# Position terms of queries and keys as sums of a row part and a column part, made on GpSimd, in the head of an attention kernel

## The chip, the cores and the metric

The kernel runs on one core of one Trainium2 chip. The core has five engines that run side by side, each through its own list of instructions in order: TensorE (PE, matrix products into PSUM), VectorE (DVE), ScalarE (ACT), GpSimd (POOL) and SyncE (SP, which here only issues DMAs). The metric is device microseconds from start to end of one execution; the median of several executions is the time of a kernel.

## The reference, cut to what matters

The input x is 8 images of 128 channels by 48 × 48 pixels, N = 2304 positions. Layer 0 normalises each image by groups of channels, appends 32 position channels to the 128 channels, and makes queries, keys and values with one linear map each and a leaky rectifier. Causal attention over the 2304 positions follows, its result is added to x. Layer 1 is a second attention without a mask on normalised tokens, and then a recurrent feed-forward part.

```python
pe = _pos_embeddings(S)            # 32 x 48 x 48: px depends on the row alone, py on the column alone
x0 = concatenate([_gn(x), pe], axis=1).reshape(B, C + 32, N)
q = lrelu(einsum('kc,bcn->bkn', Wq, x0) + bq[None, :, None])
k = lrelu(einsum('kc,bcn->bkn', Wk, x0) + bk[None, :, None])
v = lrelu(einsum('vc,bcn->bvn', Wv, x0) + bv[None, :, None])
attn = einsum('bkn,bkm->bnm', q, k) / sqrt(128)
...
x = x + out1                       # then layer 1: full attention, feed-forward, recurrence
```

The linear map over 160 channels splits into one over the 128 image channels and one over the 32 position channels and the bias. The second is the same for all 8 images. It is called the position term here. In a position channel the value depends either on the row of the pixel or on its column, so the position term at pixel (r, w) is

term(r, w) = term(r, 0) + term(0, w) − term(0, 0).

## The kernel before

**Tiling.** An image is held as a tile of 128 channels × 2304 positions. It is worked through in NQ = 6 chunks of QC = 384 positions (8 rows of 48 pixels). All numbers are fp32. One matrix product in the program appears in the profile as two MATMUL records, each with its own weight load (LDWEIGHTS, engine PEld), so that a count of x2 there is one product.

**The head.** Before the first image's attention can start, the program loads x (L716, three pieces of two chunks each through `load_x`), the position channels `pe` with a row of ones (33 rows, in two halves `pe_sb[0]` and `pe_sb[1]`) and the weights. PE starts with 12 products of the identity matrix with itself (`idle`, L1505), whose result nobody reads. They keep PE busy until the first data is there. `group_norm` computes the mean and variance of the image in three parts: BATCH_NORM_STATS2 of each chunk as x arrives (L805), then a product that averages over the channels of a group (L813), then a second such product for the variance (L824) and the reciprocal root on POOL (`rsqrt`, L669). Only then can DVE normalise the first chunk (xn, L892), and PE can multiply it by the weights (pj, L899 and L902).

**Position terms.** `positions(n, j)` makes the position term of chunk n for queries (j = 0), keys (j = 1) or values (j = 2). For j < 2 it is one product of 33 rows with 384 columns (L847). For j = 2, where the layout is turned, it is three products of 128 columns (L850). ACT copies the result from PSUM to an SBUF tile `pb` (L851). After j = 2 the whole tile is also stored to DRAM as `posb_d` (L853), from where images 1 to 7 load it. So these 18 steps are done once, in the head. Chunk 0 comes before the statistics of x, the terms of chunk 1 for q and k come behind the variance product, and chunks 2 to 5 are the steps of a chain called `making`.

**Projection.** `project(b, n)` is a chain of steps: normalise a chunk (L892), then for q, k and v a product into PSUM (L899, L902), an addition of the position term on DVE (L906), and the leaky rectifier on DVE (L907). A last step measures the largest q and k (L921).

**Attention.** For each chunk of queries and each block of 128 keys there is a product s (L1038), the exponential on ACT (L1040), for blocks on the diagonal a multiplication by the triangle mask on POOL (`triu`, L1043), and a product o with the values (L1049), which is issued LAG = 3 blocks later. DVE sums the exponentials (L1060, L1064).

**What sets the order.** The program is written under a manual schedule: the instructions of each engine run in the order of the Python calls. A planner (`Stream`) decides that order. It holds chains of steps, each with a cost on PE and a list of costs on other engines, and keeps a clock `st.now` that every product moves forward. After each attention block `st.tick()` runs up to two steps whose planned time has come. `st.advance` and `st.finish` run a chain's steps at once. An engine waits at each instruction for its inputs and for a free buffer, and everything behind it on that engine waits too. PSUM tiles called `s` have four buffers, and tiles called `t` two.

Of the kernel before, what the change touches and what calls it, by code (L numbers as in the profile page):

```python
# [14 lines left out]
F32 = mybir.dt.float32  # L15
AF = mybir.ActivationFunctionType
# [6 lines left out]
NPE = 2 * EMB  # L23
# [581 lines left out]
def fast_path(ctx: ExitStack, tc: tile.TileContext, x, pe, w_ffn, out, x_tok, w_qkv, w_pos, v_t, gamma_beta, flag):  # L605
    nc = tc.nc
    B, C, H, W = x.shape
    N = H * W
    P = 128
# [3 lines left out]
    QC = 384  # L613
    NQ = N // QC
    QB = QC // P
    SCALE = 1.0 / math.sqrt(P)
    US = 4 / 2400.0
# [10 lines left out]
    wx = cpool.tile([P, LS, B, SEGS], F32, tag="wx", name="wx")  # L628
# [42 lines left out]
    with ExitStack() as actx:  # L671
# [16 lines left out]
        def psum_s(name):  # L688
            return ps_s.tile([P, CH], F32, tag="s", name=name)

        def psum_t(name):
            return ps_t.tile([P, CH], F32, tag="t", name=name)
# [19 lines left out]
        def load_x(b, pieces=(3, 3)):  # L712
            xbuf[b] = big.tile([P, N], F32, tag="x", name=f"x_{b}")
            at = 0
            for n in pieces:
                nc.sync.dma_start(xbuf[b][:, ds(at, n * QC)], x_v[b, :, ds(at, n * QC)])  # L716
                at += n * QC

        load_x(0, (2, 2, 2))


        cg = C // GROUPS
# [67 lines left out]
        st = Stream()  # L790
# [7 lines left out]
        def group_norm(b):  # L798
            xt = xbuf[b]
            c = {}  # L800

            def part1():
                gs = small2.tile([P, NQ, 6], F32, tag="gn_st", name=f"gn_st_{b}")
                for j in range(NQ):
                    nc.vector.bn_stats(gs[:, j, :], xt[:, ts(j, QC)])  # L805
                mv = small2.tile([P, 2], F32, tag="gn_mv", name=f"gn_mv_{b}")
                nc.vector.bn_aggr(mv, gs)
                c["mv"] = mv

            def part2():  # L810
                mv = c["mv"]
                tp = psum_t(f"gn_m_{b}")
                nc.tensor.matmul(tp[:, 0:1], grp, mv[:, 0:1], start=True, stop=True)  # L813
                mg = small2.tile([P, 1], F32, tag="gn_mg", name=f"gn_mg_{b}")
                nc.vector.tensor_copy(mg, tp[:, 0:1])
                d = small.tile([P, 1], F32, tag="gn_d", name=f"gn_d_{b}")
                nc.vector.tensor_sub(d, mv[:, 0:1], mg)
                e = small2.tile([P, 1], F32, tag="gn_e", name=f"gn_e_{b}")
                nc.vector.scalar_tensor_tensor(e, d, d, mv[:, 1:2], ALU.mult, ALU.add)
                c["mg"], c["e"] = mg, e  # L820

            def part3():
                tp = psum_t(f"gn_v_{b}")
                nc.tensor.matmul(tp[:, 0:1], grp, c["e"], start=True, stop=True)  # L824
                rs = small2.tile([P, 1], F32, tag="gn_rs", name=f"gn_rs_{b}")
                rsqrt(small2, rs, tp[:, 0:1], 1e-5, "gn")
                norm_of[b] = c["mg"], rs

            return [(part1, 0.0, [("DVE", 3.6), ("", 5.0 if b else 0.0)]), (part2, 0.15, [("DVE", 0.6), ("", 2.0 if b else 0.0)]), (part3, 0.15, [("DVE", 0.15), ("POOL", 0.9)])]
# [6 lines left out]
        def positions(n, j):  # L836

            if j == 0:
                if n > 3:
                    st.advance(projected[0, n - 4], 4)  # L840
                pool, tag = ((pbp, "pb"), (pbp, "pb"), (tpool, "t"), (gpool, "g"))[n % 4]
                tile_n = pool.tile([P, 3 * QC], F32, tag=tag, name=f"pb_0_{n}")
                pos[0, n] = made[n] = tile_n.rearrange("p (j c) -> p j c", j=3)
            pe_c = pe_sb[n // (NQ // 2)][: NPE + 1, ts(n % (NQ // 2), QC)]
            ps = psum_s(f"pb_{n}_{j}")
            if j < 2:
                nc.tensor.matmul(ps[:, :QC], wpT[: NPE + 1, j, :], pe_c, start=True, stop=True)  # L847
            else:
                for m in range(0, QC, P):
                    nc.tensor.matmul(ps[:, ds(m, P)], pe_c[:, ds(m, P)], wpT[: NPE + 1, j, :], start=True, stop=True)  # L850
            nc.scalar.copy(made[n][:, j, :], ps[:, :QC])  # L851
            if j == 2:
                nc.sync.dma_start(posb_d[:, n], made[n])  # L853

        def load_positions(b, n):
            def f():
# [645 lines left out]
        def idle(tp, n):  # L1502

            for _ in range(n):
                nc.tensor.matmul(tp[:, :P], ident, ident, start=True, stop=True)  # L1505

        idle(psum_s("idle"), 12)
        for j in range(3):
            positions(0, j)
        gn = st.add(group_norm(0))  # L1510
        idle(psum_s("idle_m"), 2)
        st.advance(gn, 2)
        idle(psum_s("idle_e"), 4)
        st.finish(gn)
        for j in range(2):
            positions(1, j)
        project(0, 0)
        st.advance(projected[0, 0], 4)
        st.advance(projected[0, 1], 1)
        positions(1, 2)  # L1520
        making = st.add([(partial(positions, n, j), QC * US, [("ACT", 0.5)]) for n in range(2, NQ) for j in range(3)], 6.0)


        LAG = 3
# [38 lines left out]
    with ExitStack() as rctx:  # L1563
# [91 lines left out]
        for t in range(-WARM, LS):  # L1655
            s = t % TZ
# [98 lines left out]
```

## Time and profile before

| what | value |
|---|---|
| median of 3 executions | 1719.08 us (1713.53, 1719.08, 1719.97) |
| profiled execution | 1715.02 us |
| its span in the profile | 1713.3 us |
| PE busy, share of span | 99% |
| DVE, ACT, POOL busy | 71%, 40%, 26% |
| granted PE clock | 0.995 of full speed |
| PE products L847 in the trace | 12 (24 records) |
| ACT copies L851 | 18, mean 478 ns |

How to read it: the span is the time from the first to the last instruction that the profile shows. The execution's time lies 1.7 us above it. A busy share of 99% on PE means that almost any work taken off PE in a stage where PE is busy shortens that stage, as long as nothing else is late. The table has no time by stage, so the head must be read from the timeline and from windows of the trace.

### The profile page before, as it was taken

The numbers are of one execution on the slowest core, as the hardware profiler recorded it, in microseconds if no ns is written. First come the engines' busy times: TensorE is split into PE (matmuls) and PEld (weight loads), VectorE is DVE, ScalarE is ACT, GpSimd is POOL, SyncE is SP. The second block draws the span as 40 slices with busy tenths as digits, with TensorE's granted clock in tenths as the row PEclk, the third lists the DMA queues.
The fourth block names the chain that finished last, engine by engine and source line by source line (L and its number), as shares of the span: only waits on it lengthen the run. The fifth ranks groups of instructions, "written<-read, shape, count | busy, mean of one in ns | idle before, by whom it ended". The sixth has DMA issues, their size and how long they took to land.

```text
span 1713.3 us, 22451 instructions
## 1 busy us (share of the span) xinstructions
PE 1687.8 (99%) x6259; PEld 1085.4 (63%) x6259; DVE 1209.1 (71%) x3297; ACT 684.8 (40%) x1300; POOL 449.9 (26%) x637
## 2 busy tenths in 40 slices
PE   9999999999999999999999999999999999999986
PEld 5666666666666666666666666666666666666665
DVE  5875578666886578865787568865798657974467
ACT  3344334433344324443244333443244442443355
POOL 1233122312133122322124112331213221341205
PEclk9999999999999999999999999999999999999998
DMA  3337763568445774368735684448743686347857
GB/s 122 101 89 210 225 200 109 131 193 251 129 129 145 238 230 128 79 189 244 205 101 130 199 252 139 125 130 244 227 146 71 176 244 207 81 96 211 237 221 223
DMA packets 316731, 291.67 MB, mean 170 GB/s; under 512 B 195793, under 2 KB 280690, under 8 KB 315956
## 3 DMA queue, kind: packets, MB, share of 16 engines
q1 hardware_dynamic: 306572, 268.76, 54.7%
q0 software_dynamic: 9792, 20.99, 4.5%
q8 instruction: 52, 0.85, 0.2%
q14 instruction: 83, 0.68, 0.1%
q10 hardware_dynamic: 232, 0.40, 0.1%
HBM read 164.13 MB, written 125.90 MB: 169 GB/s over the span
## 4 chain that ended last, share of the span: by engine, by line
PE 96%; DMA 2%; DVE 1%; SPq 0%; issue 0%; ACT 0%; DVEq 0%; ACTq 0%
PE s L1038 17%; PE s L1316 17%; PE o L1049 17%; PE o L1341 17%; PE o L1329 13%; PE pj L899 3%; PE pj L902 2%; PE o L1337 2%; PE z L1666 2%; PE wx L1424 2%; DMA g<-e 1%; PE of_t L957 1%; PE pb L847 0%; PE idle_last L1505 0%; DMA x<-in_x_dram 0%; DMA e<-t 0%
## 5 line engine op out<-in xcount | busy, mean ns | idle before, releaser
L1318 ACT ACTIVATE p<-s,shift 128x384 f32<-128x384 f32 (+2 forms) x504 | 274.2, 550 | 535.9 <-PE s L1316 436.8
L1040 ACT ACTIVATE p<-s 128x384 f32<-128x384 f32 (+2 forms) x504 | 229.4, 460 | 400.1 <-PE s L1038 323.6
L1038 PE MATMUL s<-q,k 128*128 128x384 f32 (+2 forms) x1008 | 380.6, 459 | 0.1
L1316 PE MATMUL s<-xh 128*128 128x384 f32 (+2 forms) x1008 | 379.2, 458 | 0.0
L1049 PE MATMUL o<-p,vT 128*128 128x384 f32 (+2 forms) x1008 | 377.5, 456 | 0.0
L1341 PE MATMUL o<-p,xhT 128*128 128x384 f32 (+2 forms) x1008 | 369.1, 456 | 0.0
L1281 DVE STREAM_TRANSPOSE t<-p 128x384 f32<-128x384 f32 x360 | 186.0, 553 | 170.8 <-DMA e<-t 106.3
L1329 PE MATMUL o<-g,xhT 128*128 128x384 f32 x720 | 282.2, 489 | 0.7 <-DMA g<-e 0.7
L1341 PEld LDWEIGHTS o<-p,xhT 128*128 128x128 f32 x1008 | 189.7, 190 | 120.3
L1049 PEld LDWEIGHTS o<-p,vT 128*128 128x128 f32 x1008 | 186.9, 190 | 109.9 <-POOL p L1043 2.0
L1316 PEld LDWEIGHTS s<-xh 128*128 128x128 f32 x1008 | 183.2, 191 | 99.6 <-issue 0.2
L1038 PEld LDWEIGHTS s<-q,k 128*128 128x128 f32 x1008 | 183.4, 190 | 99.0 <-issue 2.2
L1064 DVE TENSOR_TENSOR acc<-acc,p 128x384 f32<-128x384 f32 (+2 forms) x408 | 212.5, 521 | 23.1 <-DVE acc L1064 1.0
L1329 PEld LDWEIGHTS o<-g,xhT 128*128 128x128 f32 x720 | 132.6, 191 | 80.2 <-DMA g<-e 2.2
L1043 POOL TENSOR_TENSOR p<-p,triu 128x128 f32<-128x128 f32 x144 | 71.3, 497 | 356.1 <-ACT p L1040 355.8
L1266 POOL DMA_DIRECT2D gm<-m x192 | 105.3, 555 | 179.1 <-PE s L1316 63.2
L1262 POOL DMA_DIRECT2D m<-tm x48 | 29.9, 623 | 374.5 <-DVE tm L1249 374.5
L1138 POOL TENSOR_SCALAR xhT<-xhT 128x384 f32<-128x384 f32 x48 | 60.5, 1260 | 150.5 <-DVE yt L1150 121.2
L1249 DVE STREAM_TRANSPOSE tm<-p 128x256 f32<-128x256 f32 x96 | 33.9, 366 | 73.1 <-ACT p L1318 72.3
L899 PE MATMUL pj<-xn,wT 128*128 128x384 f32 x192 | 77.9, 488 | 1.5 <-DVE xn L892 1.5
L947 POOL TENSOR_TENSOR rs_c<-ve_c,mhalf 128x3 f32<-128x3 f32 x48 | 48.2, 1004 | 96.1 <-DVE ve_c L941 86.8
L906 DVE TENSOR_TENSOR q<-pj,pb 128x384 f32<-128x384 f32 x48 | 26.6, 554 | 50.1 <-PE pj L899 50.1
(256 smaller groups left out, 1681.1 us busy)
## 6 DMA issues: line engine op xcount, KB each, us to landing
e<-t SPq DMA_DIRECT2D x480, 144.0 KB
g<-e SPq DMA_DIRECT2D x120, 576.0 KB
pb<-posb_d SPq DMA_DIRECT2D x42, 576.0 KB
t1t<-in_x_tok_dram SPq DMA_DIRECT2D x48, 192.0 KB
m<-tm POOLq DMA_DIRECT2D x48, 192.0 KB, 4.3
gm<-m POOLq DMA_DIRECT2D x192, 48.0 KB, 3.8
t_d<-tt SPq DMA_DIRECT2D x184, 48.0 KB
t2x<-t_d SPq DMA_DIRECT2D x46, 192.0 KB
```

Source lines behind the costliest of these rows:

```text
L899: nc.tensor.matmul(ps[:, :QC], wT[:, j, :], xn, start=True, stop=True)
L1038: nc.tensor.matmul(s[:, off:QC], keys[b][:, ts(m, P)], queries[b, j][:, off:], start=True, stop=True)
L1040: nc.scalar.activation(p[:, off:], s[:, off:QC], AF.Exp, scale=SCALE)
L1043: nc.gpsimd.tensor_mul(p[:, off : off + P], p[:, off : off + P], triu)
L1049: nc.tensor.matmul(o[:, off:QC], vals[b][:, ts(m, P)], p[:, off:], start=first, stop=last)
L1064: nc.vector.tensor_add(a[:, off:], a[:, off:], p[:, off:])
L1266: nc.gpsimd.dma_start(gm[ts(r, SQ)].rearrange("c a q r -> c a (q r)"), d.rearrange("(a c) b f -> b c a f", a=R)[r])
L1281: nc.vector.transpose(t[:, :, :, g, :].rearrange("p b j r -> p j b r"), p.rearrange("p (j b r) -> p j b r", j=QB, b=R))
L1316: nc.tensor.matmul(s[:, off:QC], xh[:, ts(m, P)], xh[:, j * QC + off : (j + 1) * QC], start=True, stop=True)
L1318: nc.scalar.activation(p[:, off:], s[:, off:QC], AF.Exp, bias=shift)
L1329: nc.tensor.matmul(out_ap, xhT[:, QB * i + g, :], p, start=first, stop=last)
L1341: nc.tensor.matmul(o[:, off:QC], xhT[:, what[1], :], p[:, off:], start=first, stop=last)
```

## The change

`load_x` of the first image uses pieces of two, two, one and one chunks. A new function `separate` makes the parts of the sum, with PE products of 24 and 48 columns. Its results are kept in the beginning of the tile `wx`, which is otherwise first written by the feed-forward part of image 0. For chunks 1 to 5 and j < 2, `positions` no longer issues a product and a copy. It issues one addition on GpSimd, in which the row part is repeated along each row and the column part is repeated for each of the 8 rows. Chunk 0, and j = 2 of all chunks, stay as they were. The two idle products between the third `positions(0, j)` and the mean product (`idle_m`) go. Six idle products (`idle_r`) come behind the variance product. The calls of `positions` for q and k of chunks 1, 2 and 3 are moved ahead: chunk 1 ahead of the group norm, chunk 2 behind the variance, chunk 3 behind the first two projections. In `making`, the steps of chunks 4 and 5 with j < 2 cost nothing on PE and 1.0 us on POOL in the planner's account, and those of chunks 2 and 3 are empty.

```diff
-        load_x(0, (2, 2, 2))
+        load_x(0, (2, 2, 1, 1))
...
+            if j < 2 and n:
+                rows = by_row[:, j, ds((n - 1) * RC, RC)].unsqueeze(2).to_broadcast([P, RC, W])
+                columns = by_column[:, j, :].unsqueeze(1).to_broadcast([P, RC, W])
+                nc.gpsimd.tensor_add(made[n][:, j, :].rearrange("p (r w) -> p r w", w=W), rows, columns)
+                return
             pe_c = pe_sb[n // (NQ // 2)][: NPE + 1, ts(n % (NQ // 2), QC)]
...
+        RC = QC // W
+        flat = wx.rearrange("p l b s -> p (l b s)")
+        n = (NQ - 1) * RC
+        by_row = flat[:, : 2 * n].rearrange("p (j r) -> p j r", j=2)
+        by_column = flat[:, ds(2 * n, 2 * W)].rearrange("p (j w) -> p j w", j=2)
+
+        def separate(h):
+
+            ps = psum_t(f"pos_parts_{h}")
+            n = H // 2
+            parts = ps[:, : 2 * (n + W)].rearrange("p (j k) -> p j k", j=2)
+            for j in range(2):
+                first = pe_sb[h][: NPE + 1].rearrange("e (r w) -> e r w", w=W)[:, :, 0]
+                nc.tensor.matmul(parts[:, j, :n], wpT[: NPE + 1, j, :], first, start=True, stop=True)
+                if h == 0:
+                    nc.tensor.matmul(parts[:, j, n:], wpT[: NPE + 1, j, :], pe_sb[0][: NPE + 1, :W], start=True, stop=True)
+            if h:
+                nc.scalar.copy(by_row[:, :, n - RC :], parts[:, :, :n])
+                return
+            corner = small2.tile([P, 2], F32, tag="qk", name="pos_corner")
+            nc.scalar.activation(corner, parts[:, :, n], AF.Copy, scale=-1.0)
+            for j in range(2):
+                nc.scalar.activation(by_column[:, j, :], parts[:, j, n:], AF.Identity, bias=corner[:, j : j + 1])
+            nc.scalar.copy(by_row[:, :, : n - RC], parts[:, :, RC : n])
...
         idle(psum_s("idle"), 12)
+        separate(0)
         for j in range(3):
             positions(0, j)
+        for j in range(2):
+            positions(1, j)
         gn = st.add(group_norm(0))
-        idle(psum_s("idle_m"), 2)
         st.advance(gn, 2)
         idle(psum_s("idle_e"), 4)
         st.finish(gn)
+        idle(psum_s("idle_r"), 6)
         for j in range(2):
-            positions(1, j)
+            positions(2, j)
         project(0, 0)
         st.advance(projected[0, 0], 4)
+        separate(1)
         st.advance(projected[0, 1], 1)
         positions(1, 2)
-        making = st.add([(partial(positions, n, j), QC * US, [("ACT", 0.5)]) for n in range(2, NQ) for j in range(3)], 6.0)
+        for j in range(2):
+            positions(3, j)
+        def making_of(n, j):
+            if j == 2:
+                return partial(positions, n, j), QC * US, [("ACT", 0.5)]
+            return (partial(positions, n, j), 0.0, [("POOL", 1.0)]) if n > 3 else (lambda: None, 0.0, [])
+
+        making = st.add([making_of(n, j) for n in range(2, NQ) for j in range(3)], 6.0)
```

## The prediction

> **What bounds the kernel now.** I read the page first, then busy time by windows, then the chain of waits and the timeline of the first 60 us. The order of instructions in the changed kernel differs from the old one only in about the first 100 us; from there on it is the same on every engine. So the head alone decides. PE's line of the page (busy tenths in 40 slices of the span) and the windows (length; then PE, PE weight loads, DVE, ACT, POOL busy; granted clock; DMA share; GB/s):
>
> ```profile
> PE   9999999999999999999999999999999999999986
> ...
> 17.10:47.00 29.90, 29.85 (x114) 17.02 (x115) 16.92 (x38) 11.28 (x26) 3.87 (x8) 1.00 0.31 115
> 47.00:56.00 9.00, 8.30 (x35) 5.25 (x33) 8.54 (x26) 2.73 (x6) 1.32 (x2) 1.00 0.34 92
> 56.00:90.00 34.00, 33.78 (x123) 21.60 (x124) 32.17 (x86) 11.20 (x25) 10.32 (x12) 1.00 0.47 122
> ```
>
> From 17 to 47 us PE is never idle, while DVE is busy 57%, ACT 38%, POOL 13%. So PE bounds the stage that holds the products of chunks 2 to 5. From 47 us on DVE is busy 95% (8.54 of 9, 32.17 of 34), so little can go wrong there. The chain in that stage (start, length, what):
>
> ```profile
> 22.11 0.86 PE pb L850 x6
> 22.97 0.65 PE pb L847 x2
> 23.61 0.84 PE s L1038 x2
> 24.46 0.65 PE o L1049 x2
> 25.10 0.84 PE pb L847 x2
> 25.94 0.84 PE pj L899 x2
> 26.79 0.65 PE s L1038 x2
> ```
>
> A product of 384 columns takes 0.65. It takes 0.84 where it follows a product with another number of rows (33 after 128, or 128 after 33): 0.19 for the switch. The timeline's PE and POOL rows in the head (in brackets the idle time before a row and what ended it):
>
> ```profile
> 9.57 0.35 PE L813 MATMUL gn_m<-gn_mv,grp 128*128 128x1 f32 x2 [0.54 <-DVE gn_mv L807]
> 11.32 0.58 POOL L669 TENSOR_TENSOR gn_rs<-ve_gn,mhalf 128x1 f32<-128x1 f32 x1 [5.33 <-DVE ve_gn L668]
> 17.15 0.91 PE L899 MATMUL pj<-xn,wT 128*128 128x384 f32 x2 [0.54 <-DVE xn L892]
> 56.22 0.88 PE L899 MATMUL pj<-xn,wT 128*128 128x384 f32 x2 [0.92 <-DVE xn L892]
> ```
>
> Before 17 us the statistics of x and then DVE bound; later PE waits only once, 0.92 at 56.2. POOL and DVE operations by line (minimum/median/maximum in ns):
>
> ```profile
> L1043 POOL TENSOR_TENSOR p<-p,triu x144: 443/455/832, 17.2 to 1503.9; 128x128 f32<-128x128 f32 x144
> L1646 POOL TENSOR_TENSOR r<-y,t2s x18: 1277/1848/2457, 1669.2 to 1693.5; 128x512 f32<-128x512 f32 x18
> L892 DVE TENSOR_SCALAR xn<-x,gn_mg,gn_rs x48: 434/471/479, 11.9 to 1459.8; 128x384 f32<-128x384 f32 x48
> L907 DVE SCALAR_TENSOR_TENSOR k<-k x48: 557/558/847, 15.1 to 1471.7; 128x384 f32<-128x384 f32 x48
> ```
>
> [...](1277 − 443) / 384 = 2.17 ns[...]. [...]the rectifier (two inputs) reaches 847 where it meets POOL, xn stays at 479. [...]The trace shows the load hidden between two 128-row products, and 0.19 lost at each switch.
>
> **The change part by part.**
>
> *Products of chunks 2 to 5, q and k.* Eight products go: 8 × 0.65 = 5.2. Seven stand between 128-row products and take two switches with them: 14 × 0.19 = 2.7. The eighth (22.97 above) stands behind an L850 group, whose switch stays. Sum −7.9, all on the path between 17 and 47. Ten ACT copies of 0.478 go too; ACT is 38% busy there, worth nothing.
>
> *Chunk 1's two products* stand at 11.04 for 1.48, while DVE and POOL finish the variance. Six idle products replace them: 12 records of 0.125 (idle_e: 8 in 1.00) are 1.5. Nothing.
>
> *Statistics.* Only one chunk's statistics (0.55) are left behind the last piece of x, so the mean product could start at 9.0 instead of 9.57, if the smaller pieces land as well as the large ones. But PE isn't free: it starts on position products at 6.20, `separate(0)` puts 8 records ahead, and chunk 0's block takes 2.12 (6.20 to 8.32, where idle_m starts). Small records aren't in the trace with 33 rows; nearest are L850's, 0.86 / 6 = 0.14 each. 6.20 + 1.15 + 2.12 = 9.47: −0.1. Bounds: 0.07 a record gives −0.5, 0.2 gives +0.4.
>
> *POOL ahead of the root.* The sums of chunk 1 now stand ahead of the root at 11.32. Four ACT operations come first[...]. One sum: 443 + 256 × 2.17 = 1.0. Both end at 10.5, 0.7 before the root needs POOL: nothing. With the contended 1.37 (1848 scaled the same way) they end at 11.2, still nothing; at 1.8 the root is 0.9 late.
>
> *POOL behind the root.* Sums of chunk 2 fill 11.9 to 13.9, those of chunk 3 start after `separate(1)` and its copy, near 15.8, and end near 18. They meet the rectifiers of chunk 0 (q at 14.03, k at 15.09, v at 16.15), which reach 0.85 instead of 0.56 when they meet POOL. One and a half such meetings ahead of the product at 17.15: +0.4 (0 to +1.2, with xn slowed too). The masks of chunk 0 queue behind: the first ends near 18.8 instead of 17.7. Its product o stood at 24.30 and will stand near 22.4: 3.6 of slack. The sums of chunks 4 and 5 lie between later masks, which have three blocks of lag, about 4 us. Chunk 4 waits for the store of chunk 0, issued near 10; DMA showed that burst at 9.75 to 11.25.
>
> *`separate(1)`*: 4 records, 0.57, ahead of the first s. PE waits 0.54 for xn at 17.15 and 0.13 before s at 15.70: hidden. Without that cover +0.6.
>
> *SP.* One more issue of x (0.41) stands ahead of the second half of `pe`, needed only near 15. The six stores wait for a tile's last writer, still the j = 2 copy. Nothing.
>
> *The wait at 56.2.* xn of chunk 4 moves forward on DVE (15 places earlier) and PE finds it ready. But DVE remains 95% busy and may be late elsewhere: −0.4 (−0.9 to 0).
>
> Sum: −7.9 − 0.1 + 0.4 − 0.4 = −8.0, with bounds of −9.8 and about −5.3. The profiled execution took 1715.0 (span 1713.3 and 1.7 around it), so it would take 1707.0. The median shown, 1719.1, lies 4.1 above it; the four executions known (1713.5, 1715.0, 1719.1, 1720.0) have their middle at 1717.1, and I take that as the kernel's level: 1709.
>
> **Rivals.**
>
> *DVE takes over.* The 16.9 us of DVE work between 17 and 47, plus about 1 of contention, must fit in 22: 82%, with q, k and v each needing a product, an addition and a rectifier in turn. For it: DVE is at 95% right behind, and what it can't finish piles up there. Against: walking the new order through with these durations, DVE reaches xn of chunk 3 near 31, and PE needs it near 34.5. If half of the gain is given back: 1717 − 4 = 1713. Chance 0.18.
>
> *The sums are slow.* Their inputs are repeated views (stride zero), which no row shows. GpSimd has forms far off the line: its power of 128 × 3 takes 1.0 us. With X a sum, the first mask ends at 8.5 + 2X + 0.58 + 4X + 0.45 once the sums delay the root; it is needed at 22.4. At X = 3.5 it is 8 late, which eats the gain. At 5.5 it ends at 42.5, 20 late: 1717 − 8 + 20 = 1729. Slower from X = 5 on. For it: nothing but the unseen form. Against: 512 plain elements take at most 2.46. Chance 0.07.
>
> *The forecast*: 0.75.
>
> **How the numbers follow.** The forecast with its bounds (−9.8 to −5.3) and 3 us of scatter to either side covers 1704 to 1715; DVE taking over reaches to 1717, and a little more below gives 1703 to 1717. Half a per cent of 1719.1 is 8.6 (about what a measurement of this kernel can tell from no change): faster means under 1710.5, slower over 1727.7. Of the forecast 0.7 lies below 1710.5 (0.53), of DVE's case 0.25 (0.05): 0.58 faster, 0.35 the same, 0.07 slower.
>
> **What would show it.** In the changed profile: L847-type PE rows only twice (chunk 0); ten POOL sums of 1.0 to 1.4; the mean product within 0.3 of 9.5; the first product of chunk 1 at 17 to 18; the last position product of chunk 5, before at 42.1, near 38.5 (it also moves behind other work); the product at 56.2 near 48.5 without a wait. I am wrong if PE shows idle time behind DVE between 18 and 40, if sums take over 2 us, or if the head ends 8 us earlier and the whole does not.

## The result, and the profile after

The changed kernel took 1708.85 us (median of 10 executions, 1705.88 to 1712.56) beside 1714.71 of the kernel before on the same chip (10 executions, 1711.96 to 1719.97). The medians differ by 5.9 us. The ratio on record, with its interval, is 0.9957 (0.9943 to 0.9970), which is not the ratio of the two medians (0.9966): 7.4 us less, with bounds of 5.1 and 9.8. The interval lies wholly below 1, so the change is a gain. It is a little under the half per cent from which the prediction spoke of "faster"; it had given 0.58 to that and 0.35 to "the same". The forecast of the time was 1709.

The profiled execution of the changed kernel has a span of 1710.8 us, against 1713.3 before. It took 1712.56 us, the longest of the ten. Part of the reason is in its head, as experiment e1 shows.

The stage from 17 to 47 us, by windows (length; then PE, weight loads, DVE, ACT, POOL busy; granted clock; DMA share; GB/s), in the changed kernel:

```profile
17.10:47.00 29.90, 28.99 (x135) 19.77 (x134) 26.30 (x54) 9.49 (x22) 10.39 (x15) 1.00 0.40 140
47.00:56.00 9.00, 9.00 (x32) 5.61 (x31) 8.62 (x28) 3.33 (x7) 2.21 (x3) 1.00 0.10 22
56.00:90.00 34.00, 34.00 (x125) 21.52 (x124) 31.05 (x85) 11.96 (x26) 9.93 (x10) 1.00 0.48 128
```

DVE is busy 26.3 of 29.9 us in the first window, 88%, where it was 57% before. DVE work that stood behind 47 us has moved forward into this window (the normalisation xn of chunk 4, for example, from 55.60 to 43.46 in e1 below). PE still never waits from 23 us to 90 us. The wait of 0.92 at 56.2 us is gone.

The chain of waits in the same place as before (start, length, what; the line numbers are those of the changed kernel, where L850 is L855 and L1038 is L1068):

```profile
23.63 0.86 PE pb L855 x6
24.49 0.84 PE s L1068 x2
25.33 0.65 PE o L1079 x2
25.98 0.70 PE pj L929 x2
26.68 0.65 PE s L1068 x2
```

From the group L855 to the next pj there are now one product s and one product o. Before, two position products of the L847 kind stood in this piece too (22.97 and 25.10 in the chain shown there).

The timeline of the head (PE and POOL rows) in the changed kernel:

```profile
8.48 1.61 POOL L847 TENSOR_TENSOR pb<-wx 128x384 f32<-128x384 f32 x2 [2.46 <-ACT wx L883]
9.81 0.58 PE L813 MATMUL gn_m<-gn_mv,grp 128*128 128x1 f32 x2
10.25 2.05 PE L1535 MATMUL idle_e<-ident 128*128 128x128 f32 x8
12.80 0.58 POOL L669 TENSOR_TENSOR gn_rs<-ve_gn,mhalf 128x1 f32<-128x1 f32 x1 [2.71 <-DVE ve_gn L668]
20.75 0.91 PE L929 MATMUL pj<-xn,wT 128*128 128x384 f32 x2 [0.91 <-DVE xn L922]
```

Two things are off the forecast. The idle products idle_e take 2.05 us for 8 records, and took 1.14 before. The first product of chunk 1 stands at 20.75 us and not at 17 to 18, and it waits 0.91 for xn. By operation (count: minimum/median/maximum in ns):

```profile
L847 POOL TENSOR_TENSOR pb<-wx x10: 819/884/1142, 8.5 to 35.5; 128x384 f32<-128x384 f32 x10
...
L922 DVE TENSOR_SCALAR xn<-x,gn_mg,gn_rs x48: 436/469/984, 13.4 to 1456.5; 128x384 f32<-128x384 f32 x48
...
L937 DVE SCALAR_TENSOR_TENSOR q<-q x48: 557/558/855, 17.0 to 1462.0; 128x384 f32<-128x384 f32 x48
```

The sums take 0.82 to 1.14 us, with a median of 0.88 where 1.0 was forecast. xn, which was said to stay at 479 ns, reaches 984.

### The profile page after: what moved, and what is told of

Its sections match the earlier page's. It is cut to its first block, busy times and chain, and to the rows that moved or that the text cites. A ratio compares the mean times of both kernels' runs of the same rounds, so it can differ in the third digit from the quotient of the medians.

```text
span 1710.8 us, 22456 instructions
## 1 busy us (share of the span) xinstructions
PE 1685.3 (99%) x6259; PEld 1088.9 (64%) x6259; DVE 1210.8 (71%) x3297; ACT 682.3 (40%) x1295; POOL 460.8 (27%) x647
## 4 chain that ended last, share of the span: by engine, by line
PE 96%; DMA 2%; DVE 1%; issue 0%; SPq 0%; ACT 0%; POOL 0%; DVEq 0%; ACTq 0%; POOLq 0%
PE s L1068 17%; PE o L1079 17%; PE s L1346 17%; PE o L1371 17%; PE o L1359 12%; PE pj L929 3%; PE pj L932 2%; PE o L1367 2%; PE wx L1454 2%; PE z L1707 1%; DMA g<-e 1%; PE of_t L987 1%; DMA e<-t 0%; DVE r L1687 0%; PE idle_last L1535 0%; PE dn L1127 0%
## 5 line engine op out<-in xcount | busy, mean ns | idle before, releaser
L1068 PE MATMUL s<-q,k 128*128 128x384 f32 (+2 forms) x1008 | 380.1, 459 | 0.0
L1068 PEld LDWEIGHTS s<-q,k 128*128 128x128 f32 x1008 | 183.9, 190 | 97.8
```

The costliest lines, as they stand in the source:

```text
L1068: nc.tensor.matmul(s[:, off:QC], keys[b][:, ts(m, P)], queries[b, j][:, off:], start=True, stop=True)
```

## The experiments

**How they are read.** The instructions of the kernels differ only in the head. Behind the first product of chunk 1, PE is without gaps up to the first product s of layer 1 (s<-xh), but for the 0.92 at 56.2 in the kernel before. So the start of that s is a landmark for what the head cost. It is the first of the two times in these rows (before, the changed kernel, and e1 below):

```profile
L1316 PE MATMUL s<-xh x42: 272/486/569, 112.5 to 139.3; 128*128 128x384 f32 x34, 128*128 128x256 f32 x4, 128*128 128x128 f32 x4
L1346 PE MATMUL s<-xh x50: 273/486/569, 107.2 to 139.0; 128*128 128x384 f32 x42, 128*128 128x256 f32 x4, 128*128 128x128 f32 x4
L1346 PE MATMUL s<-xh x54: 273/486/569, 104.6 to 139.6; 128*128 128x384 f32 x46, 128*128 128x256 f32 x4, 128*128 128x128 f32 x4
```

With one more digit they are 112.54, 107.24 and 104.58. The rest, from the landmark to the end of the span, is 1596.5 to 1603.6 us in all fourteen profiles. It has a mean of 1599.4 in the four profiles with the head of the kernel before and of 1599.7 in the ten with the new head. So no loss after the landmark shows, but the ±3.5 us of the rest hides a head that is 1 us better from a median of six executions. For this reason the landmark decides below wherever less than 2 us is in question.

All in one table, times in us; the ratio is that to the kernel before on the same chip. The landmark and the columns beside it come from one profiled execution each. "Half clock" is the stretch of the head that the trace gives with a granted PE clock of 0.50.

| kernel | median | ratio, interval | mean product | chunk 1's first pj | landmark | half clock |
|---|---|---|---|---|---|---|
| before | 1714.71 | | 9.57 | 17.15 | 112.5 | none |
| after | 1708.85 | 0.9957 (0.9943 to 0.9970) | 9.81 | 20.75 | 107.2 | 9.2 to 16.0 |
| e1_after_again | 1707.34 | 0.9953 (0.9935 to 0.9971) | 9.36 | 18.09 | 104.6 | none |
| e2_products_back | 1713.34 | 0.9985 (0.9976 to 0.9993) | 10.27 | 19.88 | 114.2 | 11.6 to 15.0 |
| e3_memset_for_sums | 1708.36 | 0.9958 (0.9945 to 0.9971) | 9.32 | 18.07 | 104.5 | none |
| e4_x_in_three | 1709.84 | 0.9962 (0.9949 to 0.9975) | 9.99 | 20.80 | 107.3 | 9.2 to 16.0 |
| e5_sums_aside | 1706.28 | 0.9951 (0.9934 to 0.9968) | 9.84 | 20.36 | 106.8 | 9.8 to 16.7 |
| e6_chunk_0_behind | 1705.29 | 0.9944 (0.9926 to 0.9962) | 9.83 | 19.20 | 106.3 | 13.8 to 17.3 |
| e7_pieces_alone | 1713.34 | 0.9993 (0.9982 to 1.0004) | 8.87 | 16.47 | 111.9 | none |
| e8_before_look | one execution | | 9.88 | 17.46 | 112.8 | none |
| e9_no_fillers | 1715.36 | 1.000 (0.999 to 1.001) | 9.85 | 20.47 | 115.8 | 8.9 to 19.2 |
| e10_idle_m_back | 1708.97 | 0.9959 (0.9943 to 0.9975) | 10.81 | 20.53 | 107.0 | 9.7 to 13.1 |
| e11_mixed_head | 1707.05 | 0.9953 (0.9940 to 0.9967) | 9.68 | 19.29 | 106.3 | 14.1 to 17.5 |
| e12_fillers_between | 1708.90 | 0.9966 (0.9953 to 0.9979) | 10.45 | 19.22 | 105.7 | none |

Two profiles of the kernel before (before and e8) differ by 0.3 at the mean product and at the landmark, and by nothing between the two. That is the scatter of a head at full clock, as far as two profiles show it.

**e1: the changed kernel again.** No edit. Is the half clock of the first profile part of the change, or does it come and go?

> The changed kernel again, for a second profile and for the granted clock of each execution. Theory A (half clock by chance): [...]some executions have it and some don't; those with a mean clock of 0.994 or more take about 3 us less than those with 0.992. Theory B (half clock by the change): the new order in the head always brings it, and every execution shows it. In either case the ratio to before is 0.995 to 0.997.

The head stayed at full clock this time, and the landmark came 2.7 earlier (104.58 instead of 107.24) with the same program. The half clock is not in every execution (A), and it costs about 2.7. Up to 0.3 of that may come from the very start: the idle products stand 0.21 apart until 5.80 us in the first profile and until 5.17 in this one, and 0.11 apart from then on, and `separate(0)` starts at 6.50 and 6.20. This profile is the one that can be laid beside the kernel before, which also had full clock. Its timeline in the head:

```profile
8.90 0.32 DVE L807 BATCH_NORM_AGGREGATE gn_mv<-gn_st 128x2 f32<-128x36 f32 x1
9.36 0.35 PE L813 MATMUL gn_m<-gn_mv,grp 128*128 128x1 f32 x2
11.69 1.72 POOL L847 TENSOR_TENSOR pb<-wx 128x384 f32<-128x384 f32 x2
11.75 0.98 DVE L922 TENSOR_SCALAR xn<-x,gn_mg,gn_rs 128x384 f32<-128x384 f32 x1 [0.69 <-POOL gn_rs L669]
15.89 1.93 POOL L847 TENSOR_TENSOR pb<-wx 128x384 f32<-128x384 f32 x2 [2.48 <-ACT wx L877]
16.46 0.67 DVE L937 SCALAR_TENSOR_TENSOR vT<-vT 128x384 f32<-128x384 f32 x1
17.06 0.98 DVE L922 TENSOR_SCALAR xn<-x,gn_mg,gn_rs 128x384 f32<-128x384 f32 x1
18.09 0.91 PE L929 MATMUL pj<-xn,wT 128*128 128x384 f32 x2 [0.91 <-DVE xn L922]
```

Both xn that PE waits for stand behind sums on POOL and take 0.98 instead of 0.48 and 0.47, and the rectifier of vT takes 0.67 instead of 0.56. Their excess, 0.50 + 0.51 + 0.11 = 1.12, is what the stretch from the mean product to chunk 1 lost: 18.09 − 9.36 = 8.73 against 17.15 − 9.57 = 7.58, which is 1.15. This stretch is 7.58 to 7.60 in the three full-clock profiles without sums (before, e7, e8), and 8.73 to 8.77 in the three of the new head (e1, e3, e12).

In all fourteen profiles, wherever an xn of the first 60 us is lengthened by a sum or a mask on POOL that started ahead of it, it ends 0.21 to 0.22 us after that POOL operation has ended (the first one here: the sum ends at 12.51 and xn at 12.73). Not every POOL operation does this. Later in e1 an xn runs wholly beside the addition of a constant on POOL and keeps its length:

```profile
57.65 1.58 POOL L1164 TENSOR_SCALAR t1t<-t1t 128x384 f32<-128x384 f32 x1
58.42 0.45 DVE L922 TENSOR_SCALAR xn<-x,gn_mg,gn_rs 128x384 f32<-128x384 f32 x1
```

**e2: eight products back.** The changed kernel, with the sums left in place and a product of 33 rows by 384 columns put back where each of the eight position products of chunks 2 to 5 stood. Nobody reads their results.

```diff
-            return (partial(positions, n, j), 0.0, [("POOL", 1.0)]) if n > 3 else (lambda: None, 0.0, [])
+            def again():
+                if n > 3:
+                    positions(n, j)
+                pe_c = pe_sb[n // (NQ // 2)][: NPE + 1, ts(n % (NQ // 2), QC)]
+                nc.tensor.matmul(psum_s(f"again_{n}_{j}")[:, :QC], wpT[: NPE + 1, j, :], pe_c, start=True, stop=True)
+            return again, 0.0, [("POOL", 1.0)] if n > 3 else []
```

> The eight products of chunks 2 to 5 are put back at their old places on PE, into PSUM tiles that nobody reads; the sums on GpSimd stay. Theory P (the products were the gain): from the first product of chunk 1 to the first s of layer 1 it takes 8 us longer than in the changed kernel (86.5 there, 95.4 in the kernel before), so 94 to 95, and the whole is 7 to 9 us slower than the changed kernel. Theory O (the new order on DVE and the wait at 56.2 were the gain): 2 us longer or less, and the whole stays within 3 us of the changed kernel.

From chunk 1's first product to the landmark it took 114.2 − 19.88 = 94.3, against 104.6 − 18.09 = 86.5 in e1: 7.8 for the eight products, where the sum of the prediction said 7.9. Theory P holds. The kernel before took 112.54 − 17.15 = 95.4 for the same stretch. Of the 1.1 left over, 0.92 is the wait at 56.2, which stays away in e2 too. The products in its timeline (two records each):

```profile
25.53 0.81 PE L1564 MATMUL again<-pe,wpT 33*128 33x384 f32 x2
26.27 0.91 PE L1068 MATMUL s<-q,k 128*128 128x384 f32 x2
27.02 0.81 PE L1079 MATMUL o<-p,vT 128*128 128x384 f32 x2
27.76 0.91 PE L1564 MATMUL again<-pe,wpT 33*128 33x384 f32 x2
28.59 0.91 PE L929 MATMUL pj<-xn,wT 128*128 128x384 f32 x2
```

Starts tell more than lengths here, since a row's length overlaps the next (25.53 + 0.81 lies behind 26.27). From its start to that of the next, the extra product at 27.76, between two products of 128 rows, takes 0.83, and the one at 25.53, which stands behind position products of 33 rows, 0.74. The ratio to the kernel before is 0.9985, so most of the change's gain is these products. The median is 6.0 us above that of e1 on the same chip, a little less than the 7 to 9 that Theory P gave.

**e3: memset in place of the sums.** The position terms of q and k of chunks 2 to 5 are left out: POOL writes zeros where it made the sums.

```diff
+                if n > 1:
+                    nc.gpsimd.memset(made[n][:, j, :], 0.0)
+                    return
                 rows = by_row[:, j, ds((n - 1) * RC, RC)].unsqueeze(2).to_broadcast([P, RC, W])
```

> The position terms of q and k of chunks 2 to 5 are left out: a memset of the same tile on GpSimd, which reads no SBUF, stands in the place of each sum. Theory S (the sums block DVE): xn of chunks 0 and 1, 0.98 each in the changed kernel, go back to 0.47, the rectifiers to 0.56, and the first product of chunk 1 comes 0.7 to 1.2 us earlier at the same granted clock; the whole is about 1 us faster. Theory N (no such blocking, xn was long for another reason): xn stays at 0.98.

The landmark is that of e1 to 0.1, and the time is the same, so the 0.7 to 1.2 us that Theory S promised did not come. Nor did Theory N: one xn is back at 0.47 and the other is longer than before. DVE and POOL rows of its timeline:

```profile
11.63 1.48 POOL L848 MEMSET pb<- 128x384 f32 x4
11.71 1.63 DVE L925 TENSOR_SCALAR xn<-x,gn_mg,gn_rs 128x384 f32<-128x384 f32 x1 [0.69 <-POOL gn_rs L669]
```

Four memsets, which read nothing from SBUF, held the first xn until the last of them had ended, at 13.11: it ends at 13.34, 0.23 behind them. The second xn has no POOL work beside it here and takes 0.47. So xn is stopped by memsets on POOL as well as by additions of two tensors, and what it loses depends on how long the POOL work that started ahead of it lasts. With sums it lost 0.5 twice, here 1.15 once: the first product of chunk 1 stands at 18.07 instead of 18.09.

**e4: x in three pieces again**, as in the kernel before.

```diff
-        load_x(0, (2, 2, 1, 1))
+        load_x(0, (2, 2, 2))
```

> x of image 0 in three pieces of two chunks again, all else as changed. Theory H (PE hides it): the mean product gn_m waits for PE's position products, not for the statistics, so that it starts within 0.2 us of where it starts in the changed kernel (9.81), and the whole is the same within 1 us. Theory X (the pieces matter): the mean product is 0.4 to 0.6 later and the whole 0.5 slower.

Landmark 107.29, against 107.24 of the changed kernel in a profile with the same half-clock stretch. The mean product is 0.2 later (9.99 and 9.81). Both numbers are as Theory H has them, but its reason holds only in part. The statistics end with BATCH_NORM_AGGREGATE on DVE (`gn_mv`, L807), and in this run they end at 9.85:

```profile
9.53 0.32 DVE L807 BATCH_NORM_AGGREGATE gn_mv<-gn_st 128x2 f32<-128x36 f32 x1
9.99 0.56 PE L813 MATMUL gn_m<-gn_mv,grp 128*128 128x1 f32 x2
```

The mean product follows 0.15 later, as it does in both profiles of the kernel before, where PE waits for them. In the first profile of the changed kernel they were ready at 8.85, and PE's products came last. In e1 they ended at 9.22 and the mean product stands at 9.36, 0.15 behind them again. So with full clock too the statistics set the mean product, with PE ready little earlier: its last position product starts at 9.04, and these follow each other at 0.11. The pieces bring little because the two paths end close together.

**e7: the four pieces alone.** The same edit the other way round, in the kernel before.

```diff
-        load_x(0, (2, 2, 2))
+        load_x(0, (2, 2, 1, 1))
```

> The kernel before with one edit: x of image 0 in four pieces. There PE waits for the statistics (0.54 ahead of the mean product). Theory H: the mean product starts 0.4 to 0.5 earlier (9.1 instead of 9.57), and the whole is about 0.5 us faster than before, less than the runs can tell. Theory D (the smaller pieces land later, by their size or by the one more issue): no earlier than 9.5.[...]

```profile
8.87 0.32 PE L813 MATMUL gn_m<-gn_mv,grp 128*128 128x1 f32 x2
```

The mean product comes at 8.87 instead of 9.57 or 9.88 (the two profiles of the kernel before). The landmark, 111.86, is 0.7 to 1.0 earlier. So the pieces do bring the statistics forward, and in the changed kernel `separate(0)` stands on PE in most of the time that they free. In the median it is not to be told from nothing (0.9993, 0.9982 to 1.0004).

**e5: the sums out of the way of xn.** In the changed kernel, the sum of chunk 2 for q goes ahead of the root. The copy in `separate(1)` goes to DVE behind xn of chunk 1, so that the sums behind it start after that xn. The sum of chunk 2 for k goes last.

```diff
+        positions(2, 0)
         gn = st.add(group_norm(0))
...
-        for j in range(2):
-            positions(2, j)
...
-                nc.scalar.copy(by_row[:, :, n - RC :], parts[:, :, :n])
-                return
+                return lambda: nc.vector.tensor_copy(by_row[:, :, n - RC :], parts[:, :, :n])
...
+        rest = separate(1)
         st.advance(projected[0, 1], 1)
+        rest()
...
+        positions(2, 1)
```

> The sums on GpSimd keep out of the way of xn: the q sum of chunk 2 goes ahead of the root, and the k sum of chunk 2 and both sums of chunk 3 come behind xn of chunk 1, held there by a copy of the second row parts that DVE makes instead of ACT. Theory L (a GpSimd instruction that is under way holds xn back until it ends): both xn take 0.47 instead of 0.98, and the first product of chunk 1 stands 8.3 us behind the mean product gn_m instead of 8.7 (at full clock), so the whole is 0.3 to 0.8 faster than the changed kernel. Theory M (moving the sums only moves the block to the rectifiers and the masks): 8.7 as before, or the first s of layer 1 no earlier than 104.6 at full clock.

```profile
13.45 0.48 DVE L921 TENSOR_SCALAR xn<-x,gn_mg,gn_rs 128x384 f32<-128x384 f32 x1 [0.69 <-POOL gn_rs L669]
19.83 0.47 DVE L921 TENSOR_SCALAR xn<-x,gn_mg,gn_rs 128x384 f32<-128x384 f32 x1
20.36 0.91 PE L928 MATMUL pj<-xn,wT 128*128 128x384 f32 x2 [0.20 <-DVE xn L921]
```

Both xn are back at 0.48 and 0.47, and the rectifier of vT is at 0.56. PE's wait at chunk 1 falls from 0.91 to 0.20. The collisions are real and can be avoided (theory L). The profile had the half clock again, and the landmark (106.8 against 107.2) shows only 0.4 of the 1.1. At half clock the first xn hides: idle_r keeps PE busy until chunk 0's first product at 15.09 in the changed kernel and 15.12 here, after xn has ended in both. What e5 brings at full clock was not measured. The median, 0.9951 of the kernel before, is not to be told from the changed kernel's.

**e6: chunk 0's products behind the variance.** On top of e5, the products of chunk 0 for q and k take the place of idle_r, and four idle products stand ahead of the mean product. (`chunk_0` only makes the tile; its store now follows the product for k. Both edits are left out here.)

```diff
         separate(0)
-        for j in range(3):
-            positions(0, j)
+        chunk_0()
+        positions(0, 2)
+        idle(psum_s("idle_m"), 4)
...
-        idle(psum_s("idle_r"), 6)
+        for j in range(2):
+            positions(0, j)
```

> As e5_sums_aside, and in addition q and k of chunk 0 come behind the variance product in the place of the six idle products, with four idle products ahead of the mean product, so that PE no longer stands between the statistics and the mean product. Theory H (PE's position products hide what the smaller pieces of x bring): the mean product starts at 8.9 to 9.0 instead of 9.36, the first s of layer 1 at about 103.6 instead of 104.6 at full clock, and the whole is about 1 us faster than the changed kernel. Theory X (the statistics end there anyway): the mean product stays at 9.3 or later.

The early mean product did not come: 9.83. By its number that is Theory X, but the reason is another. DVE had the statistics ready at 8.53, but the position channels came late enough that `separate(0)` started at 7.08, and the four idle products stood in front from 8.84 to 9.8. A second delay shows in the DVE rows of its timeline:

```profile
10.15 0.16 DVE L815 COPY gn_mg<-gn_m 128x1 f32<-128x1 f32 x1 [1.63 <-PE gn_m L813]
10.34 0.35 DVE L817 TENSOR_TENSOR gn_d<-gn_mv,gn_mg 128x1 f32<-128x1 f32 x1
10.73 0.75 DVE L819 SCALAR_TENSOR_TENSOR gn_e<-gn_d,gn_mv 128x1 f32<-128x1 f32 x1
```

gn_d and gn_e, operations on one column, take 0.16 and 0.22 in the kernel before. Both read two tensors. Here the three sums ahead of the root (9.06 to 11.46) run beside them and add 0.7 to the path of the variance. The median, 1705.29, is the lowest measured. Its interval (0.9926 to 0.9962) holds that of the changed kernel's ratio.

**e8, e9, e10: what takes the clock down.** In the changed kernel idle products of 128 rows were removed, and products of 33 rows with 24 and 48 columns were added. e8 is the kernel before once more. e9 is the kernel before without the idle products around the mean product. e10 is the changed kernel with idle_m put back.

```diff
-        idle(psum_s("idle_m"), 2)
         st.advance(gn, 2)
-        idle(psum_s("idle_e"), 4)
```

(e9, in the kernel before)

```diff
         gn = st.add(group_norm(0))
+        idle(psum_s("idle_m"), 2)
```

(e10, in the changed kernel)

> The kernel before, unchanged, a second look at its head. Theory W: the granted clock in the head depends on what PE executes there, and the head of the kernel before, with products of 128 rows between the position products, keeps full clock: no stretch at half clock in the first 20 us, the first s of layer 1 at 112.5 plus or minus 0.3. Rival C (a stretch at half clock falls in the head by chance, in this kernel as in the changed one): a stretch at 0.50 of 3.4 or 6.8 us ahead of 20 us, and the landmark some 1 to 3 us late.

> The kernel before without the idle products ahead of and behind the mean product (idle_m and idle_e; idle_r does not exist here), the 12 idle products at the start stay. Theory W (the idle products of 128 rows keep the clock of the head up): a stretch at 0.50 begins between 8 and 12 us in the profile, the first s of layer 1 comes 1.5 to 3 us late (114 to 115.5 instead of 112.5), the mean clock of the executions is 0.001 to 0.002 lower and the median 1.5 to 3 us above the kernel before. Rival N (the fillers do nothing): full clock in the head, landmark within 0.5 of 112.5, same time within 1 us.

> The changed kernel with the two idle products ahead of the mean product put back, nothing else. Theory W (their removal made the head fall to half clock in part of the executions): the head of the profile stays at full clock, the mean product starts 0.25 to 0.5 later than in the changed kernel, the mean clock of the executions is 0.0005 to 0.001 higher, and the median is the changed kernel's or up to 1.5 us below it (1705.5 to 1708). Rival N: half clock in the head as in the changed kernel, or the time rises by the 0.25 to 0.5 us of the two products.

e8 has full clock, as before and e7 had. In e9 the head fell to half clock from 8.9 to 19.2 us, and the landmark came at 115.8, even later than expected. That is Theory W's sign in the profile. Its median, though, is the kernel before's to 0.1%, not 1.5 to 3 above, so over the executions the fillers cannot have mattered that much (the interval allows up to 1.7 us). For e10 the expectation was wrong: with idle_m back the head fell all the same, at 9.67. But the two products stand at 9.80 in that profile, behind the drop, so it doesn't test what they would do ahead of one. Whether the removal of idle_m is a cause stays open. By windows (columns as above), e9 and then the changed kernel:

```profile
5.50:8.90 3.40, 3.08 (x18) 2.23 (x17) 1.59 (x4) 1.23 (x3) 0.45 (x2) 1.00 0.70 222
8.90:19.10 10.20, 8.55 (x20) 5.36 (x21) 4.48 (x12) 1.16 (x3) 0.58 (x1) 0.50 0.14 58
```

```profile
5.80:9.20 3.40, 3.40 (x23) 2.74 (x23) 2.46 (x5) 1.38 (x6) 0.94 (x2) 1.00 0.65 200
9.20:16.00 6.80, 6.80 (x30) 6.27 (x29) 1.68 (x5) 0.74 (x2) 3.18 (x5) 0.50 0.21 87
```

In the second fence PE is busy 3.40 of 3.40 us ahead of the drop. By these records it is not idle time that took the clock away. The stretches at half clock in the heads last 3.41, 6.83 or 10.24 us, that is one, two or three times 3.41. The granted clock in the traces of before and after changes in the same step throughout: the full-clock stretches of 64.85 and 1611.09 us in after are 19 and 472 times 3.413, and only the last stretch, which the end of the trace cuts off, is no multiple. A piece of 3.41 us, counted from such a change, is called a window in what follows. What the window ahead of the drop held was mostly products of 33 rows in five of the eight heads that fell (in the changed kernel 2.7 of 3.4 us), and in part (about 1.5 us) in the other three. Counted over all fourteen profiles, without the products of one column and with the window taken 0.2 us ahead of the drop, the eight heads that fell had 0.57 to 1.14 us of 128-row products in the window before the drop, and no window that held had less than 1.21. The 0.2 was chosen to fit. Without it the two groups touch (0.37 to 1.14 that fell, 1.01 and more that held). It was a rule found after the fact, so the last two runs were made to test it.

A busy record may hide idle time: the products of 24 and 48 columns stand about 0.11 apart, as products of 128 columns do. So here is a second count of the first six windows of each profile. A record of 384 columns is followed by the next after 0.323 us at full clock; each record is given the same time per column (twice that at half clock). This is an estimate of the time in which columns pass. Alone it doesn't separate the groups (1.95 to 2.68 us that fell, 1.83 and more that held). Weighted by the rows out of 128 it does, and needs no shift: 0.84 to 1.24 that fell, 1.31 and more that held. So the number of rows seems to matter, but this is a fit too. The way back needs more: by the first count, windows at half clock with up to 2.47 us of 128-row products were followed by another at half clock, and windows with 2.79 or more by full clock.

**e11 and e12: 128-row products among the 33-row ones.** e12 is the plain test: five idle products within the position products of chunk 0. e11 combines e5 with a head in which only one product of chunk 0 stands ahead of the mean product.

```diff
-        for j in range(3):
+        positions(0, 0)
+        idle(psum_s("idle_m"), 5)
+        for j in range(1, 3):
             positions(0, j)
```

(e12; e11 has three idle products, and positions(0, 1) and positions(0, 2) in place of idle_r, on top of e5)

> The kernel with the sums kept aside from xn, and in its head only one 33-row product of chunk 0 (q) ahead of the mean product, with three idle products behind it; the products of chunk 0 for k and v take the place of idle_r behind the variance. Theory W (a clock window of 3.41 us in which products of 128 rows fill less than about 1.2 us drops the next to half): every window of the head now holds at least 1.5 us of them, so the head stays at full clock whatever the phase; the mean product starts at 8.8 to 9.1, the first product of chunk 1 at 17.0 to 17.8, the first s of layer 1 at 103.0 to 104.0 (the changed kernel: 104.6 at full clock, 107.2 with its half-clock stretch), the median 1 to 3 us below the changed kernel's 1708 (1705 to 1707). Rival C (the drops come by chance, or from something else than the kind of product): a stretch at 0.50 in the head again, landmark 106 or later.

> The changed kernel with five idle products of 128 rows put between the first and the second position product of chunk 0, nothing else. Theory W: no window in the head with less than 1.2 us of 128-row products, so full clock; the mean product 1.2 later than at full clock without them (10.5 to 10.7), the first s of layer 1 at 105.5 to 106.2, between the changed kernel's 104.6 and 107.2; median within 1 us of the changed kernel's. Rival C: a stretch at 0.50 in the head as in six of the eight profiles with this head so far, and the landmark at 108 to 109.

e12 did as the rule says: full clock, the mean product at 10.45, the landmark at 105.7. One profile at full clock is no proof, since e1 and e3 had it without fillers, and since the windows of e12 begin at 4.55 us, earlier than in any head that fell (4.78 to 7.30). In e11 the head fell, at 14.1, against what was expected, and the landmark came at 106.3, not at 103 to 104. PE rows of its timeline:

```profile
9.83 1.14 PE L1534 MATMUL idle_e<-ident 128*128 128x128 f32 x8
11.63 0.38 PE L824 MATMUL gn_v<-gn_e,grp 128*128 128x1 f32 x2 [0.67 <-DVE gn_e L819]
11.95 0.91 PE L852 MATMUL pb<-pe,wpT 33*128 33x384 f32 x2
12.69 0.83 PE L855 MATMUL pb<-wpT,pe 33*128 33x128 f32 x6
13.48 2.27 PE L928 MATMUL pj<-xn,wT 128*128 128x384 f32 x4
```

The variance came late (gn_e behind the sums, as in e6), and between idle_e and pj stood a wait and only 33-row products. The window before the drop held 0.90 us of 128-row work by the count above. Both runs agree with the rule. The expectation that e11 would keep every window above 1.5 was a wrong count of where the products would stand.

## Why the prediction came out right

The main term and its mechanism were right. Two smaller terms were off by about as much in opposite directions, which is luck, and one was missing. Compared at full clock, e1 against before, in us at the landmark:

| term | forecast | measured |
|---|---|---|
| products of chunks 2 to 5 with their switches | −7.9 | −7.8 (e2 against e1) |
| statistics | −0.1 | −0.2 (9.36 against 9.57; scatter 0.3) |
| collisions of POOL and DVE | +0.4 | +1.15 |
| wait at 56.2 | −0.4 | −0.9 |
| sum | −8.0 | −8.0 (104.58 against 112.54; the four terms make −7.75) |
| half clock in the head | not foreseen | about +2.7 where it comes |

*Products.* The price of 0.65 a product and 0.19 a switch, taken from the chain, was right, and so was the reading that PE bounds this stage.

*Statistics.* The number was right and the path only in part. The prediction had PE as the last to be ready, at 9.47, and the statistics in time for 9.0. In the first profile it was so (statistics at 8.85, mean product at 9.81, with half clock). In e1, from which the −0.2 is taken, PE was ready near 9.2 and the statistics came last, at 9.22, because the last piece of x came later (its statistics start at 8.30, in the first profile at 7.94).

*Collisions.* Here the step failed in size. It rested on "xn stays at 479", read as a sign that xn doesn't contend with POOL. In the kernel before, only eight of the 48 xn met work on POOL: four the last 0.12 us of a mask, four a power of three columns (`roots`). None met an addition of two large tensors or a memset, and none was held up, so the rows did not show the meeting that the change would bring. The range of the step named xn slowed too as its upper end, +1.2, and that is what came. The runs show that POOL held xn back (0.98 behind a sum in e1, 1.63 behind four memsets in e3), but not by what means, and the addition of a constant on POOL that didn't hold it back (0.45 at 58.42 in e1) is not explained.

*The wait at 56.2* is gone as a whole, so the middle between all and nothing was too careful. DVE's xn of chunk 4 moved from 55.60 to 43.46 in e1, and PE takes its product at 48.33 without a wait (forecast near 48.5):

```profile
43.46 0.47 DVE L922 TENSOR_SCALAR xn<-x,gn_mg,gn_rs 128x384 f32<-128x384 f32 x1
48.33 0.81 PE L929 MATMUL pj<-xn,wT 128*128 128x384 f32 x2
```

*The sums* took 0.80 where undisturbed (two in 1.61 at 8.18), not 1.0. The estimate from two plain forms (2.17 ns for each further column, from the shortest mask and the shortest addition of 128 × 512) was too high, and no extra cost of the repeated inputs shows. The rival of slow sums falls. Their start at 8.5, and with it their end at 10.5, was the author's estimate. In the first profile of the changed kernel the four ACT operations ahead of them (0.17, twice 0.30, 0.19) ran from 7.63 to 8.40, and the two sums from 8.48 to 10.09.

*DVE takes over* falls too. DVE is 88% busy between 17 and 47 us, and PE has no gap after chunk 1's first product up to the landmark, neither in after nor in e1. DVE's xn of chunk 3 stands at 31.58 in e1, where the prediction had it near 31.

*The bounds* of the sum, −9.8 and −5.3, don't follow from the terms that the prediction shows: its lowest values make −7.9 − 0.5 + 0 − 0.9 = −9.3, and its highest, without the cases that it sets aside, −7.9 + 0.4 + 1.2 + 0 = −6.3. The measured −8.0 lies within either pair.

*Two more signs.* The last position product of chunk 5 was forecast near 38.5, and stands at 38.07 in e1 and at 40.72 in the profile with half clock. Chunk 1's first product was forecast at 17 to 18, and stands at 18.09 and 20.75; the first is the collisions, the second the half clock.

*The level.* 1717.1 was assumed for the kernel before. On the chip of the result it took 1714.7, in the later comparisons 1713.5 to 1716.65. So the level was taken some 2.4 too high and the gain 0.6 to 2.1 too large, and the two cancel in the predicted time: that it came within 0.2 us of the measured one is luck. A half clock in part of the executions would explain why the gain is less than the 8.0 at full clock; that is not shown. Whether the change makes it more likely is not settled. Of the profiles with the new head, e12 apart, seven of nine show it, and none of the three with the unchanged position products and fillers (before, e7, e8). But those three had their clock windows at a phase (full clock from 4.62, 5.09 and 5.39 us) at which e1 and e3 held it as well (5.17, 5.21), while e2 (4.78) fell, one window later.

No version tried is clearly better than the changed kernel. e5, e6 and e11, which remove the collisions, have ratios of 0.9944 to 0.9953 with intervals that overlap its own.

## What to carry to other kernels

Where PE is without gaps, price a removed product by its place in the chain: its time and the two switches of shape around it (here 0.65 and 2 × 0.19). Here the sum held to a tenth of a microsecond. A maximum over many rows says that two operations don't disturb each other only if they met in that trace, so look for a meeting before using it. Before comparing two profiles at the level of microseconds, look at the granted clock in the stretch: one program had its landmark at 104.6 and at 107.2. Where PE's own work seems to set when a product starts, look also at when its input was ready: two paths that end close together can change places from one execution to the next (the mean product in the changed kernel's profile and in e1).

## What the runs showed of the hardware

Work on POOL can delay a DVE operation that reads only one tensor: xn (one SBUF tensor in, two scalars) goes from 0.47 to 0.98 behind sums (e1) and to 1.63 behind memsets (e3), and ends 0.21 to 0.23 us after them. The addition of a constant on POOL didn't do this (xn 0.45 at 58.42 in e1). A DVE operation on a single column, with two tensors in, went from 0.22 to 0.75 beside sums (e6). A GpSimd addition whose two inputs are repeated views of 128 × 384 takes 0.80 to 0.82 us undisturbed (e1, after).

In the changed kernel the PE clock fell to half although the records show PE busy without a gap, when most of the 3.41 us before (2.7) were products of 33 rows. Eight of the fourteen profiles have a drop in the head, and each came where 128-row products had filled 1.14 us or less of that time, while no window that held had less than 1.21. This is a fit with a chosen shift, with which the two runs made after it agree. What the chip counts isn't shown.
